# Layer 0 of a graph network: the edge-type one-hots by a broadcast load and a compare instead of a transpose on TensorE

## The chip, the cores and the metric

The kernel runs on one core of a Trainium2 chip. The metric is the time of one execution on the device in microseconds (us), as the median of several runs. The engines are named as the profile names them: PE (TensorE, matrix multiplies; PEld is its loading of weights), DVE (VectorE), ACT (ScalarE), POOL (GpSimd) and SP (SyncE, which here only issues DMAs).

## The reference

Four graph layers run one after the other on 3125 nodes of 256 features and 50,000 edges, sorted by destination. After each, the result is added to `x` and normalised. The change lies in layer 0, whose edge part is:

```python
e = edge_emb[edge_type]                       # 16 types
x_src, x_dst = node_embeddings[src], node_embeddings[dst]
att_in = concat([x_src, x_dst, e, task_rep], axis=-1)
edge_delta = tanh(gelu(att_in @ att_W1 + att_b1) @ att_W2 + att_b2)
edge_weight = 1.0 + edge_scale * edge_delta
messages = ((x_src + e) @ msg_W + msg_b) * (1.0 + 0.5 * tanh(msg_gamma)) + msg_beta
agg = segment_sum(messages * edge_weight, dst)     # then divided by the sum of edge_weight
```

Since `att_W1` acts on a concatenation, its product is a sum of a part by source, a part by destination and a part by edge type. The kernel computes the three parts per node and per type once and looks them up for each edge.

## The kernel before

**Tiles.** Edges are cut into 416 tiles (`TT`) of up to 128 edges, so that the destinations of one tile lie within one block of 128 nodes; four tiles are a group (`G`), and there are 104 groups. The function `bucket` prepares the tiles' data once: `s_src`, `s_dl` (destination within the block) and `s_ty` (type) hold one edge per partition and one tile per column. It also calls `segments`, which works on the transposed form (one tile per partition, edges along the columns) and makes the tables for the softmax of later layers. `segments` takes 128 tiles at a time, in four blocks, and collects a block's values in `pk`, one PSUM buffer of 128 x 4 x 128 float32 values, by matmuls with the selection matrix `sel`. Its third slice was used only for `kd`, one column (L380), which DVE reads as `low` (L383) before it goes on to `dl` (L388).

**One-hot matrices.** A look-up by destination is a matmul with a 0/1 matrix. `gathered` makes two of them per tile: `places[:, 0]` has a one in the column of each edge's destination (L928), and `places[:, 1]` has in columns 0 to 47 three copies of the type's one-hot over 16 types (L934, from the one made on L931), with zeros in the other 80 columns, set once (L918). PE turns both (L939), eight transposes per group into one PSUM buffer `ohp`, and ACT copies the 1024 columns to `oht` (L943). Three copies are needed since the per-type table `ec` holds its values as three bfloat16 parts under one another, 48 rows, padded with zeros to 128.

**The edge loop** runs `gathered` for one group, `attended` for the group before and `summed` for the one before that. POOL gathers the source rows into `gb` (L509, by `self.gather`). `attended` adds up the three parts in `pre` on PE: the source part by a matmul with the identity (L956, three bfloat16 parts), the destination part with `oht[:, 0]` (L961, three parts per tile), the type part with `oht[:, 1]` and `ec` (L964, one per tile). ACT applies Gelu (L965), DVE multiplies with `att_W2` and sums (L967). `summed` makes the weighted one-hots `ohw` (L972 to L976) and adds each tile's messages to `acc` (PE L979, DVE L981). The L979 matmuls are float32, all the others of the loop bfloat16.

For every second group SP stores the pair's destination one-hots and their transposes to memory (`oh_d`, `oht_d`, L946), where layers 1 and 2 load them.

**Order.** The kernel's source gives the order in which buffers are written and read; a planner with estimated costs sets the order of instructions on each engine and adds the waits. Each engine then works through its list in order. Access to a PSUM buffer is kept in order by the bank.

Of the kernel before, what the change touches and what calls it, by code (L numbers as in the profile page):

```python
# [9 lines left out]
F32 = mybir.dt.float32  # L10
# [8 lines left out]
P = 128  # L19
D = 256  # L20
# [13 lines left out]
class Net:  # L34
# [178 lines left out]
    def bucket(self, src, dst, type16, type8, weight, relations):  # L213
# [22 lines left out]
        self.seg = self.dram.tile([TT, 5, P], F32, name="seg")  # L236

        self.rows = self.dram.tile([NS, 2, S], F32, name="rows")
        self.astart, self.aend, self.anew = (c.tile([1, TT], F32, name=n) for n in ("astart", "aend", "anew"))
        self.tnode = c.tile([1, TT], I32, name="tnode")  # L240

        with tc.tile_pool(name="bk", bufs=1, side="right") as b:
# [40 lines left out]
            with tc.tile_pool(name="bkw", bufs=1, side="right") as w, tc.tile_pool(name="bkp", bufs=1, space=PSUM) as ps:  # L283
# [71 lines left out]
                nc.vector.tensor_single_scalar(bat, bat, D, op=ALU.mult)  # L355
                nc.scalar.dma_start(self.b_at, bat)

                self.segments(w, bd, nxt, prv, bdf, sel, kd)

    def segments(self, w, bd, nxt, prv, bdf, sel, kd):  # L360

        tc, nc, TT = self.tc, self.nc, self.TT
        C = bd.shape[1]
        flag = w.tile([P, 2, C, P], F32, name="flag")
        nc.vector.tensor_tensor(flag[:, 0], prv, bd, op=ALU.not_equal)
        nc.vector.tensor_tensor(flag[:, 1], nxt, bd, op=ALU.not_equal)
        zero = w.tile([P, P], F32, name="zero")
        nc.vector.memset(zero, 0.0)
        with tc.tile_pool(name="sgp", bufs=1, space=PSUM) as ps, tc.tile_pool(name="sg", bufs=2, side="right") as v:
            rows = ps.tile([1, 3, 512], F32, name="rows")  # L370
            for m0 in range(0, TT, P):
                M = min(P, TT - m0)
                pk = ps.tile([P, 4, P], F32, name="pk")
                for n in range(3):
                    for k in range(C):
                        nc.tensor.matmul(pk[:M, n, :], sel[:, k, m0:m0 + M],
                                         bdf[:, k, :] if n == 0 else flag[:, n - 1, k, :],
                                         start=k == 0, stop=k == C - 1)
                for k in range(C):
                    nc.tensor.matmul(pk[:M, 3, 0:1], sel[:, k, m0:m0 + M], kd[:, k:k + 1],  # L380
                                     start=k == 0, stop=k == C - 1)
                low = v.tile([P, 1], F32, name="low")
                nc.vector.tensor_scalar(low[:M], pk[:M, 3, 0:1], self.pidx[:M], float(m0),  # L383
                                        op0=ALU.add, op1=ALU.add)
                nc.vector.tensor_scalar(low[:M], low[:M], float(P), None, op0=ALU.mult)
                sg = v.tile([P, 5, P], F32, name="sg")
                dl = v.tile([P, P], F32, name="dl")
                nc.vector.tensor_scalar(dl[:M], pk[:M, 0, :], low[:M], None, op0=ALU.subtract)  # L388
                ins = v.tile([P, P], F32, name="ins")
                nc.vector.tensor_scalar(ins[:M], dl[:M], 0.0, None, op0=ALU.is_ge)  # L390
                nc.vector.scalar_tensor_tensor(ins[:M], dl[:M], float(P), ins[:M], op0=ALU.is_lt, op1=ALU.mult)
                nc.vector.tensor_scalar(sg[:M, 0], ins[:M], -1.0, -NEG, op0=ALU.add, op1=ALU.mult)
                for n in (1, 2):
                    nc.vector.scalar_tensor_tensor(sg[:M, n], pk[:M, n, :], NEG, ins[:M],
                                                   op0=ALU.mult, op1=ALU.mult)
                nc.vector.tensor_tensor_scan(sg[:M, 3], zero[:M], sg[:M, 1], 0.0, op0=ALU.add, op1=ALU.min)
                nc.vector.tensor_tensor_scan(sg[:M, 4, ::-1], zero[:M], sg[:M, 2, ::-1], 0.0,
                                             op0=ALU.add, op1=ALU.min)
                edge = v.tile([P, 1], F32, name="edge")
                nc.vector.tensor_add(edge[:M], sg[:M, 0, 0:1], sg[:M, 1, 0:1])  # L400
                for n, col in enumerate((sg[:M, 3, P - 1:P], sg[:M, 4, 0:1], edge[:M])):
                    nc.tensor.matmul(rows[:, n, m0:m0 + M], col, self.ident[:M, :M], start=True, stop=True)
                nc.sync.dma_start(self.seg[m0:m0 + M], sg[:M])
            for n, row in enumerate((self.astart, self.aend, self.anew)):
                nc.vector.tensor_copy(row, rows[:, n, :TT])
            rrow = w.tile([1, TT // S, 2, S], F32, name="rrow")
            nc.vector.memset(rrow, NEG)
            st, en = (r.rearrange("p (s t) -> p s t", t=S) for r in (self.astart, self.aend))
            nc.vector.tensor_copy(rrow[:, :, 0, 1:], st[:, :, :S - 1])
            nc.vector.tensor_copy(rrow[:, :, 1, :S - 1], en[:, :, 1:])  # L410
            nc.sync.dma_start(self.rows.rearrange("s n t -> (s n t)")[None, :], rrow.rearrange("p s n t -> p (s n t)"))
# [342 lines left out]
    def layer0(self, task, edge_emb, msg_W, msg_b, att_W1, att_b1, att_W2, att_b2, edge_scale,  # L754
# [9 lines left out]
        with ExitStack() as layer:  # L764
# [21 lines left out]
            ub2 = vec(up_b2, D, "ub2")  # L786
            lng = vec(ln_g, D, "lng")
            lnb = vec(ln_b, D, "lnb")
            ec = wp.tile([P, D], BF, name="ec")
            nc.vector.memset(ec, 0.0)  # L790
            one = wp.tile([P, 1], F32, name="one1")
            nc.vector.memset(one, 1.0)
            me = wp.tile([ET, D], F32, name="me")
# [2 lines left out]
            with tc.tile_pool(name="n0", bufs=2) as w, tc.tile_pool(name="m0", bufs=1) as wm, \  # L796
# [18 lines left out]

                ml = film_loads(ma_W1, ma_b1, ma_W2, ma_b2, "ma")
                ul = film_loads(ua_W1, ua_b1, ua_W2, ua_b2, "ua")
                E3 = 3 * ET
                emb = wm.tile([E3, D], F32, name="emb")
                for n in range(3):  # L820
                    nc.sync.dma_start(emb[n * ET:(n + 1) * ET, :], edge_emb)
# [58 lines left out]
                nc.vector.tensor_scalar(fst[:, 2:3], self.pidx[:E3], float(2 * ET), None, op0=ALU.is_ge)  # L880
                nc.vector.tensor_add(fst[:, 1:2], fst[:, 0:1], fst[:, 2:3])
                nc.vector.tensor_scalar(fst[:, 1:2], fst[:, 1:2], -1.0, 1.0, op0=ALU.mult, op1=ALU.add)
                nc.vector.tensor_scalar(ecs, part[:, 0, :], fst[:, 0:1], None, op0=ALU.mult)
                for n, o in ((1, ecs), (2, ec[:E3])):
                    nc.vector.scalar_tensor_tensor(o, part[:, n, :], fst[:, n:n + 1], ecs,
                                                   op0=ALU.mult, op1=ALU.add)
                nc.vector.tensor_add(me, mb[:ET, :], pc[:ET, 1, :])
# [23 lines left out]
            with tc.tile_pool(name="e0g", bufs=5) as gp, tc.tile_pool(name="e0", bufs=3) as w, \  # L911
# [1 line left out]

                places = [hp.tile([P, 2, 2, G, P], BF, name="places%d" % n) for n in range(2)]
                for n, oh in enumerate(places):
                    (nc.vector if n % 2 else nc.gpsimd).memset(oh[:, 1], 0.0)  # L918
                ohts = [None]

                def gathered(t0):
                    gb = gp.tile([P, G, ET + XA], F32, name="gb")
                    for j in range(G):
                        self.gather(gb[:, j, ET:], table, self.s_src, t0 + j)
                    g = t0 // G % 2
                    both = places[t0 // (2 * G) % len(places)]
                    oh = both[:, :, g]
                    nc.vector.tensor_tensor(  # L928
                        oh[:, 0], self.iota[:, None, :].to_broadcast([P, G, P]),
                        self.s_dl[:, t0:t0 + G][:, :, None].to_broadcast([P, G, P]), op=ALU.is_equal)  # L930
                    nc.vector.tensor_tensor(  # L931
                        gb[:, :, 0:ET], self.iota[:, None, :ET].to_broadcast([P, G, ET]),
                        self.s_ty[:, t0:t0 + G][:, :, None].to_broadcast([P, G, ET]), op=ALU.is_equal)
                    nc.vector.tensor_copy(oh[:, 1, :, 0:3 * ET].rearrange("p j (n e) -> p j n e", n=3),  # L934
                                          gb[:, :, None, 0:ET].to_broadcast([P, G, 3, ET]))
                    pt = ps.tile([P, 2, G, P], BF, name="ohp")
                    for n in range(2):
                        for j in range(G):
                            nc.tensor.transpose(pt[:, n, j, :], oh[:, n, j, :], self.idb)  # L939
                    if not g:  # L940
                        ohts[0] = hp.tile([P, 2, 2, G, P], BF, name="oht", bufs=2)
                    oht = ohts[0][:, :, g]
                    nc.scalar.copy(oht, pt)  # L943
                    if g:
                        for to, of in ((self.oh_d, both), (self.oht_d, ohts[0])):
                            nc.sync.dma_start(to[t0 // (2 * G)], of[:, 0].rearrange("p g j v -> p (g j v)"))  # L946
                    return t0, gb, oh, oht

                def attended(t0, gb, oh, oht):
                    hg = w.tile([P, G, D], F32, name="hg", bufs=2)  # L950
                    dl = w.tile([P, G], F32, name="dl")
                    for j0 in range(0, G, 2):
# [4 lines left out]
                        for j in (j0, j0 + 1):  # L957
                            q = pre[:, j - j0, :]
                            node = self.node_of(nc.tensor, t0 + j)
                            for n in range(3):  # L960
                                last = nc.tensor.matmul(q, oht[:, 0, j, :], xbr[:, ds(node * (3 * D) + n * D, D)],  # L961
                                                        start=False, stop=False)
                            self.used(nc.tensor, last)
                            nc.tensor.matmul(q, oht[:, 1, j, :], ec, start=False, stop=j > j0)  # L964
                        nc.scalar.activation(hg[:, j0:j0 + 2, :], pre, AF.Gelu)  # L965
                        for j in (j0, j0 + 1):
                            nc.vector.scalar_tensor_tensor(hg[:, j, :], hg[:, j, :], 1.0, aw2, op0=ALU.mult,  # L967
# [3 lines left out]
                def summed(t0, gb, oh, dl):  # L971
# [1 line left out]
                    nc.scalar.activation(dl, dl, AF.Identity, bias=one, scale=esc)  # L973
                    ohw = w.tile([P, G, P], F32, name="ohw", bufs=2)
                    for j in range(G):
                        nc.scalar.activation(ohw[:, j, :], oh[:, 0, j, :], AF.Copy, scale=dl[:, j:j + 1])  # L976
                    for j in range(G):
                        pa = ps.tile([P, SW], F32, name="pa", bufs=3)
                        nc.tensor.matmul(pa, ohw[:, j, :], gb[:, j, 0:ET + D], start=True, stop=True)  # L979
# [645 lines left out]
```

## Time and profile before

| what | value |
|---|---|
| time of the runs shown, median of 3 | 3369.55 us (3362.56 to 3373.93) |
| time of the profiled execution | 3362.1 us |
| its span, first to last instruction | 3360.3 us |
| mean granted TensorE clock | 0.843 of full speed |
| PE, DVE, ACT, POOL busy over the span | 80%, 68%, 43%, 54% |
| layer 0's edge loop | about 212 to 796 us, at granted clock 1.00 from 250 us on |
| transposes L939 / type matmuls L964 | 832 / 416 |
| gathers L509 in the loop | 416, mean 0.98 us |

A line such as `L964 PE MATMUL pre<-ec,oht 128*128 128x256 bf16` names the line of the kernel, the engine, what is written from what, and for PE the shape of the weights (rows*columns) and of the data that stream past them. In the timeline each line begins with the start and the length in microseconds; a group of neighbouring instructions is one line, with its number behind an x. The bracket at the end is the idle time of the engine ahead of it and what ended that; "issue" is idle time for which the profile shows no wait. Matmuls are pipelined: the length of one includes its way through the array, so what one costs PE is read from the distance of the starts.

### The profile page before, as it was taken

To read this page: it belongs to the slowest core of one execution; us is meant where nothing else is said; L and a number is where in the kernel's file an instruction comes from. 1 tells how busy PE (TensorE), PEld (TensorE's weight loads), DVE (VectorE), ACT (ScalarE), POOL (GpSimd) and SP (SyncE) were. 2 spreads that over 40 slices of the span, in tenths; PEclk is the share of its full clock that TensorE was granted. 3 is DMA by queue.
4 is the path that set the end of the run, shared out by engine and by line. 5 is a ranking of instruction groups with operands and counts; after the bars stand their busy time and mean duration, and the time that the engine had idled before them with its cause. 6 is when DMAs were issued, how large, how long until landed. Compare 5 with 4: busy or idle time off the path is not lost. (4 is left out here: it accounts for less than half of the span.)

```text
span 3360.3 us, 50557 instructions
## 1 busy us (share of the span) xinstructions
PE 2693.6 (80%) x12679; PEld 1753.9 (52%) x12679; DVE 2274.4 (68%) x6046; ACT 1446.9 (43%) x4376; POOL 1827.1 (54%) x1850
## 2 busy tenths in 40 slices
PE   2779999999979777777775847888888887888885
PEld 1357777775545345555553525666666663333332
DVE  2646666676655378988886437888888873555556
ACT  1427777774456335544543215656656562000000
POOL 4037767771044167666662556676766202777773
PEclk9889999999989878888887878888888985565656
DMA  7249988884067877777774367878777235333332
GB/s 167 72 147 295 295 284 289 287 291 137 32 252 288 311 225 244 232 230 238 228 229 136 116 206 201 225 225 227 228 226 228 76 140 215 105 105 106 106 105 86
DMA packets 240616, 658.40 MB, mean 196 GB/s; under 512 B 47960, under 2 KB 87012, under 8 KB 234013
## 3 DMA queue, kind: packets, MB, share of 16 engines
q0 software_dynamic: 132400, 484.37, 46.4%
q1 hardware_dynamic: 104262, 167.53, 15.1%
q10 hardware_dynamic: 3676, 3.23, 0.5%
q8 instruction: 122, 2.00, 0.2%
q14 instruction: 156, 1.28, 0.1%
HBM read 513.06 MB, written 151.58 MB: 198 GB/s over the span
## 5 line engine op out<-in xcount | busy, mean ns | idle before, releaser
L509 POOL DMA_INDIRECT gb<-table,s_src x832 | 852.4, 1025 | 374.8 <-issue 203.9
L706 PE MATMUL pr<-r,oh 128*128 128x260 f32 x2496 | 733.6, 440 | 80.7 <-DVE acc L711 32.9
L706 PEld LDWEIGHTS pr<-r,oh 128*128 128x128 f32 x2496 | 502.5, 217 | 216.0 <-issue 33.1
L1509 POOL DMA_INDIRECT ring<-table,b_rel x391 | 369.9, 946 | 312.8 <-DVE oh L1519 194.0
L701 ACT ACTIVATE r<-gb,ex 128x64 f32<-128x64 f32 x2080 | 522.4, 336 | 0.0
L509 POOL DMA_INDIRECT gb<-table,s_rel x416 | 405.4, 974 | 204.9 <-issue 106.0
L711 DVE TENSOR_TENSOR acc<-acc,pr 128x260 f32 (+1 forms) x832 | 457.7, 550 | 72.7 <-PE pr L706 60.8
L1538 PE MATMUL pa<-ring,oh 128*128 x832 | 428.9, 628 | 84.1 <-DMA ring<-table,b_rel 41.2
L1538 PEld LDWEIGHTS pa<-ring,oh 128*128 128x128 f32 x832 | 193.7, 283 | 319.6 <-DVE oh L1519 215.2
L1545 DVE TENSOR_TENSOR x<-x,pa 128x256 f32 x416 | 175.2, 421 | 227.0 <-PE pa L1538 225.2
L1237 PE MATMUL pqe<-q_all,oht 128*128 x1248 | 207.8, 306 | 91.9 <-DVE pd L1242 76.1
L693 ACT CAST oh<-ohb 128x512 f32<-128x512 bf16 x208 | 128.3, 618 | 307.2 <-PE pr L706 278.6
L589 ACT ACTIVATE r<-mv,eps 128x4 f32<-128x4 f32 (+3 forms) x27 | 7.9, 297 | 536.5 <-DVE mv L575 533.1
L697 DVE TENSOR_TENSOR r<-gb,ex 128x512 f32<-128x512 f32 (+1 forms) x208 | 225.8, 1086 | 12.9 <-ACT ex L666 9.2
L979 PE MATMUL pa<-gb,ohw 128*128 128x272 f32 x832 | 223.7, 402 | 5.3 <-DVE acc L981 3.8
L1237 PEld LDWEIGHTS <-oht 128*128 128x128 bf16 x1248 | 131.6, 107 | 126.8 <-issue 86.0
L961 PE MATMUL pre<-xb,oht 128*128 x1248 | 193.7, 273 | 0.0
L981 DVE TENSOR_TENSOR acc<-acc,pa 128x272 f32 x416 | 180.7, 434 | 6.2 <-PE pa L979 3.4
L928 DVE TENSOR_TENSOR places<-iota,s_dl 128x512 bf16<-128x512 f32 x104 | 72.0, 692 | 161.5 <-ACT ohw L976 161.5
L956 PE MATMUL pre<-gb,idb 128*128 128x512 bf16 x624 | 169.3, 381 | 5.3 <-DMA gb<-table,s_src 5.3
L979 PEld LDWEIGHTS pa<-gb,ohw 128*128 128x128 f32 x832 | 141.5, 190 | 55.6 <-issue 35.1
L967 DVE SCALAR_TENSOR_TENSOR hg<-hg,aw 128x256 f32<-128x256 f32 x416 | 159.4, 421 | 16.1 <-ACT hg L965 16.1
(381 smaller groups left out, 4291.6 us busy)
## 6 DMA issues: line engine op xcount, KB each, us to landing
ohb<-oh_d SPq DMA_DIRECT2D x104, 256.0 KB
oht<-oht_d SPq DMA_DIRECT2D x104, 256.0 KB
table<-row SPq DMA_DIRECT2D x25, 1024.0 KB
gb<-table,s_src POOLq DMA_INDIRECT x832, 4.5
oh_d<-places SPq DMA_DIRECT2D x52, 256.0 KB
oht_d<-oht SPq DMA_DIRECT2D x52, 256.0 KB
sgm<-seg SPq DMA_DIRECT2D x26, 320.0 KB
gb<-table,s_rel POOLq DMA_INDIRECT x416, 4.4
```

The lines of the kernel that those rows point to most:

```text
L509: self.nc.gpsimd.indirect_dma_start(out=out, out_offset=None, in_=table, in_offset=bass.IndirectOffsetOnAxis(ap=idx[:, t:t + 1], axis=0))
L697: nc.vector.tensor_mul(r[:, :, :nd, :hw], v[:, :, :nd, :], ex[:, :nd, s0:s0 + G].rearrange("p h t -> p t h")[:, :, :, None].to_broadcast([ ...
L701: nc.scalar.activation(r[:, j, h, :hw], v[:, j, h, :], AF.Copy, scale=ex[:, h, s0 + j:s0 + j + 1])
L706: nc.tensor.matmul(pr[:, n, :HB * F], oh[:, j, :], r[:, j, n * HB:(n + 1) * HB, :].rearrange("p h f -> p (h f)"), start=True, stop=True)
L711: self.used(nc.vector, nc.vector.tensor_add(a, a, pr[:, :, :HB * F]))
L961: last = nc.tensor.matmul(q, oht[:, 0, j, :], xbr[:, ds(node * (3 * D) + n * D, D)], start=False, stop=False)
L979: nc.tensor.matmul(pa, ohw[:, j, :], gb[:, j, 0:ET + D], start=True, stop=True)
L981: self.used(nc.vector, nc.vector.tensor_add(a, a, pa))
L1237: last = nc.tensor.matmul(pq[:, j, :], oht[:, j, :], q_all[:, ds(node * (3 * D) + n * D, D)], start=n == 0, stop=n == 2)
L1509: st = nc.gpsimd.indirect_dma_start(out=ring[:, at:at + D], out_offset=None, in_=table, in_offset=bass.IndirectOffsetOnAxis(ap=b_rel[:, b: ...
L1538: last = nc.tensor.matmul(pa, oh[:, j, :], ring[:, ds(at, D)], start=True, stop=True)
L1545: self.used(nc.vector, nc.vector.tensor_add(a, a, pa))
```

## The change

The transposed type one-hots are no longer made from `places[:, 1]`. `segments` now writes each tile's 128 types to memory (`ty_d`, one row per tile), taken by four more matmuls per block (L376's kind, in float32) into the slice `pk[:, 3, :]` after `low` has been read. In the loop, SP loads for each pair of groups the 1024 types, the same row into each of 48 partitions. In `attended`, DVE compares them with each partition's own type number `own` (0 to 15, three times over) in place, and the result is the weights of the type matmul: 48 rows instead of 128. `ec` and the one-hots lose their padding, `ohp` and `oht` their second half.

```diff
+        self.ty_d = self.dram.tile([TT, P], BF, name="ty_d")
...
+                for k in range(C):
+                    nc.tensor.matmul(pk[:M, 3, :], sel[:, k, m0:m0 + M], f16[:, k, :], start=k == 0, stop=k == C - 1)
+                ty = v.tile([P, P], BF, name="ty")
+                nc.scalar.copy(ty[:M], pk[:M, 3, :])
+                nc.sync.dma_start(self.ty_d[m0:m0 + M], ty[:M])
                 sg = v.tile([P, 5, P], F32, name="sg")
...
-            ec = wp.tile([P, D], BF, name="ec")
-            nc.vector.memset(ec, 0.0)
+            E3 = 3 * ET
+            ec = wp.tile([E3, D], BF, name="ec")
+            own = wp.tile([E3, 1], F32, name="own")
...
+                nc.vector.scalar_tensor_tensor(own, fst[:, 2:3], 2.0, fst[:, 1:2], op0=ALU.mult, op1=ALU.add)
+                nc.vector.scalar_tensor_tensor(own, own, -float(ET), self.pidx[:E3], op0=ALU.mult, op1=ALU.add)
...
-                places = [hp.tile([P, 2, 2, G, P], BF, name="places%d" % n) for n in range(2)]
-                for n, oh in enumerate(places):
-                    (nc.vector if n % 2 else nc.gpsimd).memset(oh[:, 1], 0.0)
-                ohts = [None]
+                both = [None]
 
                 def gathered(t0):
...
-                    both = places[t0 // (2 * G) % len(places)]
-                    oh = both[:, :, g]
+                    if not g:
+                        both[0] = [hp.tile([p, 2, G, P], BF, name=n, bufs=2) for p, n in (
+                            (P, "places"), (P, "oht"), (E3, "types"))]
+                        nc.sync.dma_start(both[0][2].rearrange("p g j e -> p (g j e)"), bass.AP(
+                            tensor=self.ty_d.tensor, offset=self.ty_d.offset + t0 * P,
+                            ap=[[0, E3], [1, 2 * G * P]]))
+                    oh, oht, ty = (b[:, g] for b in both[0])
...
-                    nc.vector.tensor_copy(oh[:, 1, :, 0:3 * ET].rearrange("p j (n e) -> p j n e", n=3),
-                                          gb[:, :, None, 0:ET].to_broadcast([P, G, 3, ET]))
-                    pt = ps.tile([P, 2, G, P], BF, name="ohp")
-                    for n in range(2):
-                        for j in range(G):
-                            nc.tensor.transpose(pt[:, n, j, :], oh[:, n, j, :], self.idb)
+                    pt = ps.tile([P, G, P], BF, name="ohp")
+                    for j in range(G):
+                        nc.tensor.transpose(pt[:, j, :], oh[:, j, :], self.idb)
...
-                def attended(t0, gb, oh, oht):
+                def attended(t0, gb, oh, oht, ty):
+                    nc.vector.tensor_scalar(ty, ty, own, None, op0=ALU.is_equal)
...
-                            nc.tensor.matmul(q, oht[:, 1, j, :], ec, start=False, stop=j > j0)
+                            nc.tensor.matmul(q, ty[:, j, :], ec, start=False, stop=j > j0)
```

## The prediction

> **What bounds the kernel now.** I looked first at the stages: where does the time go in which the changed code runs? The busy times by window (columns: PE, weight loads, DVE, ACT, POOL busy us with instruction counts, granted clock, DMA share, GB/s) give for 100 us in the middle of layer 0's edge loop:
>
> ```profile
> 450.00:550.00 100.00, 99.05 (x692) 71.76 (x690) 69.00 (x271) 71.61 (x164) 69.78 (x73) 1.00 0.89 287
> ```
>
> PE is busy 99 of 100 us at full clock; nobody else passes 72, though the DMA engines stand at 0.89. The loop runs from 212 to 796 us, 104 groups of four edge tiles. Next, the waits between 250 and 750 us (total, times, longest):
>
> ```profile
> DVE places L928 <- ACT ohw L976: 148.4, 91, 1.7
> ACT dl L972 <- DVE hg L967: 115.4, 91, 1.7
> ...
> PE pa L979 <- DVE acc L981: 2.3, 10, 0.4
> ```
>
> DVE and ACT wait once a group (91 groups, 1.6 and 1.3 us each), for one another and in the end for PE's `pre`; PE itself waits 2.3 us in 500. So a group costs what PE's instructions cost. "Busy" overlaps for pipelined matmuls, so I price by start-to-start times in PE's timeline (start, length, number):
>
> ```profile
> 500.90 2.10 PE L979 MATMUL pa<-gb,ohw 128*128 128x272 f32 x8
> ...
> 502.83 0.61 PE L939 MATMUL ohp<-idb,places 128*128 128x128 bf16 x8
> 503.28 0.81 PE L956 MATMUL pre<-gb,idb 128*128 128x512 bf16 x3
> 503.93 0.49 PE L961 MATMUL pre<-xb,oht 128*128 x3
> 504.26 0.27 PE L964 MATMUL pre<-ec,oht 128*128 128x256 bf16 x1
> 504.37 0.49 PE L961 MATMUL pre<-xb,oht 128*128 x3
> ...
> 506.32 2.10 PE L979 MATMUL pa<-gb,ohw 128*128 128x272 f32 x8
> ```
>
> A period is 506.32 - 500.90 = 5.42 us. Eight transposes take 503.28 - 502.83 = 0.45 us, 56 ns each; L964 takes 504.37 - 504.26 = 0.11 us, no more than each L961 (0.33/3). Loads of weights are hidden.
>
> **What is removed in the loop.** Four of the eight transposes: 4 x 0.056 = 0.225 us of PE per group. ACT's copy of 1024 columns (0.99 us) becomes one of 512; the nearest row, the 128x512 cast L693, has 0.62, so -0.37. DVE's cast L934 (0.27) goes. For the end this is worth nothing: both engines wait over a microsecond per group for PE, and without PE in the way DVE would still need only 5.42 - 1.65 = 3.8 us a group.
>
> **What L964 becomes.** It has 48 rows of weights instead of 128, four times a group, each time between 128-row matmuls. L964 is the step on which this forecast turns. The trace of before has no 48-row matmul, but it has 16-row and 64-row ones among 128-row ones. In layer 0's node stage (PE alone):
>
> ```profile
> 807.22 1.99 PE L1027 MATMUL pm<-sx,mw 128*128 128x512 f32 x4
> 809.14 1.12 PE L1029 MATMUL pm<-sx,me 16*128 16x512 f32 x2
> 810.19 1.42 PE L1012 MATMUL tr<-ident,acc 128*128 128x128 f32 x11
> ...
> 820.51 1.88 PE L1044 MATMUL pm<-gT,uw 128*128 128x512 f32 x4
> 822.23 1.88 PE L1044 MATMUL pm<-xT,uw 128*128 128x512 f32 x4
> ```
>
> Without a change of rows, four such matmuls take 822.23 - 820.51 = 1.72 us (0.43 each). With one they take 809.14 - 807.22 = 1.92, and the two of 16 rows 1.05 instead of 0.86: 0.2 us more per change. Half of that is a float32 weight load that is no longer pulled ahead (0.11), the rest, 0.09, is the array running empty. In bf16, in layer 1's loop, around a 64-row transpose:
>
> ```profile
> 1230.25 0.27 PE L1237 MATMUL pqe<-q_all,oht 128*128 x1
> 1230.45 0.27 PE L664 MATMUL mis<-ident,smA 64*128 64x64 f32 x1
> 1230.65 0.28 PE L1237 MATMUL pqe<-q_all,oht 128*128 x1
> 1230.78 0.41 PE L1237 MATMUL pqe<-q_all,oht 128*128 x2
> ```
>
> The bf16 matmul of 256 columns (0.11) gives way after 0.20: again 0.09 of emptying. Back at 128 rows the first bf16 matmul takes 0.12, so its exposed load costs only about 0.01. A change costs 0.10 with bf16 weights behind it and 0.09 + 0.11 = 0.20 with float32 weights.
>
> Against these rows stand two sentences of the Trainium skill. "TensorEngine Tiling (Array Packing)", Tiling Modes (Key Properties), says that a change of tiling mode drains the array; its modes have 128, 64 or 32 rows, so 48 rows would run as 64. "TensorE: Matmul & The Clock Gate", LDWEIGHTS, says that the number of rows does not matter for a load. By the second alone L964 costs its 0.11 as before; by the first and the rows it costs two changes. Both are true in the trace (16-row matmuls are no slower by themselves), and the first decides, because it is the neighbours that pay. That 48 counts as 64 no row shows; the 48-column matmul L872 is followed by a gap like the others ("issue" 0.40 before the next load), which I take as the same rounding.
>
> Per group: eight changes, 7 x 0.10 + 0.20 (the last L964 is followed by the float32 L979) = 0.90 us. With 0.225 less for transposes: **+0.67 us per group, 104 x 0.67 = +70 us**. Ends: if the 48-row bf16 weights load without the short path, each way in costs 0.20: +0.39 per group, +111 us in all; the page of the clock gate (Weight-path perf modes) ties that path to 128 columns and not float32, which L964 keeps, so I stay near the row. Below: no change of mode, -0.225 x 104 = -23.
>
> **The compare.** One per group, 48x512 bf16, on DVE ahead of L964. Nearest rows: tensor_scalar L312, 0.43 us for 416 float32 columns, and L928, 0.69 for 512; below, L390 at 0.23 for 128. I take 0.5. DVE is busy 0.69 of 5.42 = 3.7 us per group; 3.7 - 0.3 + 0.5 = 3.9 of 6.1: hidden. It waits for a load, and behind it on DVE stand `hg`, `acc` and the next one-hots, for which ACT and then PE wait: with DVE's idle time (1.65 a group now, about 2.2 then) it takes a load some 4 us late per pair of groups before PE feels it.
>
> **The load and the stores.** 52 loads of 48 rows x 2 KB on SP. The hardware queue moved 12973 packets in 500 us at 12.4% of 16 engines: 76 ns each. 48 x 76 / 16 = 0.23 us per pair, 2% of 10.84. Share 0.91 at the old pace, 0.81 at the slower one: no bound. SP issues three DMAs of 0.32 us per pair instead of two. It does stand up to 9.7 us a pair in front of the `oht_d` store, waiting for ACT; a load queued behind it leaves late, but it is asked for a group before its use, and gathers beside it land in 4.5 us. I cost it at nothing. Stores behind a load wait only for tile reuse two pairs on.
>
> **Ahead of the loop.** `segments` is on the path: the loop's first one-hot starts (211.8) after its last copies. Four blocks each get eight float32 matmuls of 128 columns, an ACT copy and a store. L376's sixteen take 1.95 us, so eight take 0.98, behind DVE's `low`; `dl` then waits, since all of `pk` is one bank (in layer 1 L644 waits for ACT's copy of another part of its bank, 24 times). `dl` starts 0.24 us after the first `low` ends; with load, eight matmuls and tail of 0.17 it starts about 1.3 after: +1.1 per block, x4 = 4.4; at half clock, as in the second block, up to 8; 0 if the planner hides it. The copy (0.4) and store lie beside DVE's 2 us. Removed: POOL's memset L918, 1.1 us in front of the first gather (0 to 1.1 won; I take 0.5). The two small DVE operations for `own` lie among node tiles: 0. Net **+4**.
>
> **Sum.** 70 + 4 = +74 us. The profiled execution took 3362.1 (span 3360.3 and 1.8 around it), so 3436; the median of the runs shown is 7.5 above it, so 3369.55 + 74 = **3444**. The bound of 0.3%, which a measurement here can tell from nothing, is 10 us.
>
> **Rivals.** (1) *48 rows change no mode.* Then -23 + 4 = -19: 3350, faster. POOL (1.22 us a gather, 4.9 a group) and DMA (0.91 x 5.42 = 4.9) allow 5.2. For it: the row-count sentence. Against it: every row-count change in the trace pays. With p for a change it wins where 8p + 0.10 + 4/104 is under 0.225: p below 0.01 us, a tenth of what the rows show. 9%. (2) *Dearer loads*, the 0.20 above: +111 + 4, 3485; 14%. (3) *Some changes are free*, say half: +0.22 per group, +23 + 4, 3397; 7%. (4) *The load lands late*: at 2 us beyond the slack, 52 x 2 = 104 more, 3548; gathers' landing speaks against it. 4%. My forecast has 66%, own range 3425 to 3465.
>
> **Range and chances.** 3395 to 3490 takes all of the first, most of (2) and part of (3): 80%. It leaves out (1) and (4). Faster 0.09, within 0.3% 0.01, slower 0.90.
>
> **What will show it.** Period of L979 about 6.1 us; the loop's stage about 70 us longer, with DVE, ACT and DMA shares down and PE still never waiting. Weight loads of the 48-row matmul and of those after it starting about 0.09 after the stream of the one before, "issue" ahead of them. Transposes 416, not 832. Blocks of `segments` a microsecond longer each. Wrong if PE's starts around the 48-row matmul stay 0.11 apart, or if PE idles for DVE's compare.

## The result

The kernel after the change takes 3430.3 us (median of four runs, 3423.0 to 3431.2), the kernel before 3368.7 (3362.6 to 3373.9): a ratio of **1.0185** (95% interval 1.017 to 1.020), 61.6 us slower. The profiled executions are 68.1 us apart (3430.2 and 3362.1), at granted clocks of 0.849 and 0.843.

In three of the five sets of runs below the kernel before itself took about 4040 us instead of 3365, since signals from TensorE reached the other engines up to 2.5 us late and TensorE no longer bounded the loop ("late signals" below); every ratio is therefore to the kernel before in its own set, and those three sets are read for TensorE's start-to-start times more than for their totals.

### The profile after

The stage first: busy times by window, for the same 100 us of the edge loop as in the prediction (PE, weight loads, DVE, ACT, POOL, then granted clock, DMA share, GB/s).

```profile
450.00:550.00 100.00, 99.93 (x563) 58.03 (x563) 66.48 (x247) 56.74 (x150) 73.67 (x66) 1.00 0.87 268
```

PE is still the bound, with 563 matmuls in 100 us instead of 692. From the first L986 (L979 before) to the end of the last one the loop takes 624.3 us (239.7 to 864.0) instead of 567.2, and the median distance between groups is 6.03 us instead of 5.43. Next, PE's own timeline of one group (start, length):

```profile
504.07 0.28 PE L971 MATMUL pre<-ec,types 48*128 48x256 bf16 x1
504.29 0.50 PE L968 MATMUL pre<-xb,oht 128*128 x3
504.72 0.28 PE L971 MATMUL pre<-ec,types 48*128 48x256 bf16 x1
504.93 0.82 PE L963 MATMUL pre<-gb,idb 128*128 128x512 bf16 x3
...
506.66 0.28 PE L971 MATMUL pre<-ec,types 48*128 48x256 bf16 x1
506.87 0.50 PE L986 MATMUL pa<-gb,ohw 128*128 128x272 f32 x1
```

Behind each type matmul (L971, L964 before) the next one starts 0.21 us later, where it was 0.11; ahead of it the last L968 takes 0.205 until L971 starts. The waits between 300 and 780 us (total, times, longest) say what PE's weight loads sit idle for, and whether PE waits for anyone:

```profile
ACT hg L972 <- PE pre L971: 105.5, 79, 1.3
...
PEld L971 <- issue: 66.7, 317, 0.2
...
DVE types L956 <- DMA types<-ty_d: 49.1, 40, 1.8
...
PEld pa L986 <- issue: 5.2, 12, 0.7
...
PE pa L986 <- DVE acc L988: 0.3, 1, 0.3
```

Ahead of each of 317 loads of 48-row weights PEld idles 0.21 us, with no wait to blame. DVE waits 1.2 us per pair of groups for the types' load (40 pairs), and PE feels little of it: the loads for L986 stand idle 12 times, and by the starts of L986 every second distance is longer than 6.03 by 0.09 us in the mean, 4.5 us in the whole loop.

By the first L986 10.3 us more have passed than before by the first L979: 1.9 before `segments` starts (I have no cause for it; over all the traces kept that moment lies anywhere between 174.5 and 183.3 us), 7.8 in `segments` from its first matmul to the last `dl` (36.0 instead of 28.2), the rest at the loop's start. The timeline of one block of `segments`:

```profile
183.72 1.16 PE L389 MATMUL pk<-f,sel 128*128 128x128 f32 x8
...
184.91 0.27 ACT L391 CAST ty<-pk 128x128 bf16<-128x128 f32 x1 [7.10 <-PE pk L389]
...
185.21 0.35 DVE L395 TENSOR_SCALAR dl<-pk,low 128x128 f32<-128x128 f32 x1 [1.25 <-ACT ty L391]
```

DVE's `dl` waits not only for the eight type matmuls, but also for ACT's copy out of the same bank. After the loop nothing changed (2563.6 us before, 2564.4 after).

### The profile page after: what moved, and what is told of

Read it like the earlier page. It is cut to its first block, busy times and chain, and to the rows that moved or that the text cites. A ratio compares the mean times of both kernels' runs of the same rounds, so it can differ in the third digit from the quotient of the medians.

```text
span 3428.4 us, 49867 instructions
## 1 busy us (share of the span) xinstructions
PE 2753.0 (80%) x12295; PEld 1708.0 (50%) x12295; DVE 2293.7 (67%) x6046; ACT 1394.9 (41%) x4380; POOL 1876.9 (55%) x1849
## 5 line engine op out<-in xcount | busy, mean ns | idle before, releaser
L516 POOL DMA_INDIRECT gb<-table,s_src x832 | 902.5, 1085 | 519.1 <-issue 210.7
L986 PE MATMUL pa<-gb,ohw 128*128 128x272 f32 x832 | 222.9, 407 | 1.4 <-DVE acc L988 1.2
L968 PE MATMUL pre<-xb,oht 128*128 x1248 | 207.2, 275 | 0.0
L972 ACT ACTIVATE hg<-pre 128x512 f32<-128x512 f32 x208 | 123.5, 594 | 146.0 <-PE pre L971 146.0
L986 PEld LDWEIGHTS pa<-gb,ohw 128*128 128x128 f32 x832 | 145.8, 189 | 46.8 <-issue 7.3
```

The lines of the kernel that those rows point to most:

```text
L516: self.nc.gpsimd.indirect_dma_start(out=out, out_offset=None, in_=table, in_offset=bass.IndirectOffsetOnAxis(ap=idx[:, t:t + 1], axis=0))
L968: last = nc.tensor.matmul(q, oht[:, j, :], xbr[:, ds(node * (3 * D) + n * D, D)], start=False, stop=False)
```

## The experiments

Theory M is the prediction's: every 48-row matmul among 128-row ones costs two changes of row mode. Theory L says that the types' load, the comparison or the DMA traffic costs the time; theory S says `segments` does. Rival G, for the versions with a faster TensorE, says that the gathers would then be late.

### The type matmul alone cut to 48 rows

```diff
-                            nc.tensor.matmul(q, oht[:, 1, j, :], ec, start=False, stop=j > j0)
+                            nc.tensor.matmul(q, oht[:3 * ET, 1, j, :], ec[:3 * ET], start=False, stop=j > j0)
```

> The kernel before, with one thing of the change alone: the type matmul (L964) takes the first 48 rows of its weights and of ec; transposes, copies, casts and segments stay. Theory M (each 48-row matmul among 128-row ones is two changes of row mode, about 0.10 us each, eight per group): the median distance of two L979 starts goes from 5.43 to 5.43 + 0.82 = 6.25 us, and the time, less some 5 us that the first groups already lose to late gathers, from 3369 to about 3450 (3440 to 3457). Theory L (the time is lost to the types load, its comparison on DVE or the extra DMA traffic, none of which is in this kernel): 3369 and 5.43. Theory S (the segments' extra work is the main cost): 3369.

Measured: ratio 1.0003 (0.9975 to 1.003), in a set where the kernel before took 4040 us. What went on there is seen best in its 80-row sister, whose expectation was:

> As the 48-row version of the kernel before, but with 80 rows, of which rows 48 to 79 are zero as before. Theory M with 48 rows running as a 64-row mode and 80 as the full 128: no change of mode, 3369 us and a distance of 5.43. Rival M' (any row count other than 128 empties the array on both sides): the same as 48 rows, about 3450 and 6.25. Theory L or S: 3369, so this run only says which row counts pay.

The edit is the same with `5 * ET`; the ratio is 0.9986 (0.9962 to 1.001). From the timeline of this 80-row kernel, one group:

```profile
502.45 0.27 PE L964 MATMUL pre<-ec,oht 80*128 80x256 bf16 x1
...
502.56 1.54 PE L979 MATMUL pa<-gb,ohw 128*128 128x272 f32 x6
...
505.27 0.60 ACT L965 ACTIVATE hg<-pre 128x512 f32<-128x512 f32 x1 [2.52 <-PE pa L979]
505.32 0.44 DVE L981 TENSOR_TENSOR acc<-acc,pa 128x272 f32 x1 [1.62 <-PE pa L979]
```

L964 was done at 502.7, yet ACT, idle, starts on its result at 505.27; in the trace of before the same hand-over took 0.04 us. DVE starts at the same moment on a result that PE had finished at 503.2. PE has run out of buffers meanwhile. A group takes 7.40 us here in both kernels. Where signals are prompt (below) it takes 5.43 with 128 rows and 6.25 with 48, so what M adds is spent inside a wait here. Busy times by window, first the kernel with 80 rows, then with 48:

```profile
450.00:550.00 100.00, 74.85 (x509) 52.97 (x507) 56.00 (x201) 52.89 (x121) 51.07 (x54) 1.00 0.69 212
```

```profile
450.00:550.00 100.00, 88.03 (x512) 49.89 (x511) 55.85 (x200) 53.11 (x122) 51.58 (x55) 1.00 0.69 212
```

PE is 13 us of 100 busier for the same work and the same pace. The start-to-start times are clean: with 48 rows 0.205 us into the type matmul and 0.212 out of it (medians of 416 and 208), with 80 rows 0.109 and 0.113. So 80 rows beside 128 change no mode, and 48 do. This agrees with the Trainium skill, "TensorEngine Tiling (Array Packing)", Tiling Modes (Available Configurations), where the modes have 128, 64 or 32 rows; its Key Properties name the drain, and the price, 0.10 us each way, comes from these rows. A rival, that the 48-row loads are merely not pulled ahead, would make the way out longer where a longer load follows; it is 0.21 us before the bf16 loads (98 ns) and before the float32 ones (190 ns) alike. The totals of this pair decide nothing between M and L. A repetition, with its expectation:

> The same kernel as k48_alone (before, with the type matmul alone cut to 48 rows), since on the first chip signals from TensorE reached the other engines late and TensorE waited in both kernels. On a chip where the kernel before takes about 3369 us, theory M expects what it did: a distance of 6.25 us, and about 3450 us (3440 to 3457); theories L and S: 3369. On a chip where the kernel before takes about 4040 us again, theory M expects no difference in time, and TensorE about 0.8 us a group busier.

came out under the same condition: 1.0005 (0.9978 to 1.0032), distance 7.41.

### The same with the gathers left out

The next two runs were meant to make TensorE the bound again under late signals.

```diff
+                gbs = [gp.tile([P, G, ET + XA], F32, name="gb%d" % n, bufs=1) for n in range(5)]
...
-                    gb = gp.tile([P, G, ET + XA], F32, name="gb")
-                    for j in range(G):
-                        self.gather(gb[:, j, ET:], table, self.s_src, t0 + j)
+                    gb = gbs[t0 // G % 5]
+                    if t0 < 5 * G:
+                        for j in range(G):
+                            self.gather(gb[:, j, ET:], table, self.s_src, t0 + j)
```

> The kernel before with 396 of layer 0's 416 gathers left out: the five buffers of gathered rows are filled once and used again and again, so layer 0's sums are of the wrong rows; every other instruction of the loop stays. In the seven traces of this kind of chip TensorE's signals are late (by up to 2.5 us, several at once) only in stretches where GpSimd issues gathers. If the gathers bring that on, the loop is bound by TensorE again: 5.42 us from L979 to L979, a loop of about 104 x 5.42 = 564 us instead of 760, and a time of about 4043 - 196 = 3847 (3835 to 3860). If the signals are late whatever GpSimd does, the distance stays at 7.4 and the time near 4043, and no kernel of this study can be bound by TensorE on such a chip.

The condition had passed: the kernel before took 3360.9 us in this set and this kernel 3363.2, ratio 0.9998 (0.9984 to 1.0012). So whether gathers bring on the late signals stays open; what the run shows is that layer 0's gathers cost the kernel before little. Its loop is 8 us shorter (559.1), and that is not a late start: of the 8.5 us that the kernel before loses against 5.43 us a group, the first ten distances hold 1.6, and nearly all of it lies in every second distance, all through the loop. There DVE's first `acc` of a group starts late, behind the sequencer's reading of the next node numbers:

```profile
L523 DVEq TENSOR_LOAD <-tnode x87: 339/345/1006, 302.0 to 775.2; - x87
```

The three numbers are the shortest, the median and the longest in ns (300 to 780 us); without the gathers none is over 345 there. In every second distance of the kernel before, the distance follows the length of this read (correlation 0.94).

> The kernel few_gathers_before (396 of layer 0's 416 gathers left out, so the sums are of the wrong rows) with the type matmul cut to 48 rows. few_gathers_before took 0.9998 of the kernel before (3363 and 3361 us), so the gathers are hidden there, and leaving them out keeps the loop bound by TensorE whether signals are prompt or late. Theory M: 5.43 + 0.82 = 6.25 us from group to group, 104 x 0.82 = 86 us, 1.0253 of few_gathers_before: 3448 us where the kernel before takes 3361 (3440 to 3455). Theories L (load, comparison or traffic of the types) and S (segments): 3363, since none of that is in this kernel.

Measured: **1.0250** (1.0233 to 1.0267) of the kernel before, and so 1.0252 of few_gathers_before by way of its 0.9998, where 1.0253 was expected; the distance is 6.25 us in nearly every group, against 5.43. The groups of the type matmul between 300 and 780 us (busy, mean ns, idle before), first with 128 rows, then with 48:

```profile
L967 PE MATMUL pre<-ec,oht 128*128 128x256 bf16 x354 | 96.5, 273 | 0.0
L967 PEld LDWEIGHTS <-oht 128*128 128x128 bf16 x354 | 34.7, 98 | 4.0
```

```profile
L967 PE MATMUL pre<-ec,oht 48*128 48x256 bf16 x306 | 85.6, 280 | 0.0
L967 PEld LDWEIGHTS <-oht 48*128 48x128 bf16 x306 | 28.3, 93 | 64.4 <-issue 64.4
```

Matmul and load are as long as before; only the 0.21 us of idle time ahead of each load is new. M alone gives more than the whole loss of the change (the loop is 83 us longer than in few_gathers_before), and there is no load, no comparison and no extra work in `segments` here. L and S are out as the main cause; what is left of L in the kernel after is the 4.5 us above, and of S the 7.8.

### The two 48-row matmuls of a pair put together

```diff
                             self.used(nc.tensor, last)
-                            nc.tensor.matmul(q, ty[:, j, :], ec, start=False, stop=j > j0)
+                        for j in (j0, j0 + 1):
+                            nc.tensor.matmul(pre[:, j - j0, :], ty[:, j, :], ec, start=False, stop=j > j0)
```

> The kernel after, with the two 48-row matmuls of each pair of tiles put behind one another (after the one-hot matmuls of both tiles), so that a group has four changes of row mode instead of eight. Theory M: 4 x 0.105 = 0.42 us less per group, a distance of 5.61 instead of 6.03, and 3430 - 44 = 3387 us (3380 to 3395). If instead each 48-row matmul has a price of its own, whatever stands beside it, the time stays near 3430. Theory L: 3430.

Under late signals: 0.9936 (0.9908 to 0.9964). PE's starts were as M says: 0.205 into the first of the two, 0.119 between them, 0.202 out. Then again:

> The same kernel as paired (after, with the two 48-row matmuls of a pair of tiles one behind the other, four changes of row mode a group instead of eight). Where the kernel before takes about 3361 us, theory M: 5.61 us from group to group and 3423 - 0.42 x 104 = 3379 us (3372 to 3386), 1.0033 to 1.0075 of the kernel before; theory L: 3423, 1.0185. Where it takes about 4040: 0.9936 again.

1.0095 (1.0074 to 1.0117). Even distances (from the first group to the second, from the third to the fourth, and so on) are 5.61 us, exactly as expected: 0.42 less with four changes of mode fewer, so the price belongs to the change and not to the matmul. But the gain in time, 0.9% or 30 us, is short of the expected 44. (That it is about half of the whole loss is chance, since the loss has other terms too.) Odd distances say where the rest is: 5.88 in the median and 5.95 in the mean, 0.34 x 51 = 17 us. Once per pair something else is now the limit. The last kernel of the next section shows it plainly.

### Every matmul on 128 rows

```diff
-            ec = wp.tile([E3, D], BF, name="ec")
+            ecp = wp.tile([P, D], BF, name="ec")
+            nc.vector.memset(ecp, 0.0)
+            ec = ecp[:E3]
...
+                types = [hp.tile([P, 2, G, P], BF, name="types%d" % n) for n in range(2)]
+                for ty in types:
+                    nc.vector.memset(ty, 0.0)
...
-                    nc.vector.tensor_scalar(ty, ty, own, None, op0=ALU.is_equal)
+                    nc.vector.tensor_scalar(ty[:E3], ty[:E3], own, None, op0=ALU.is_equal)
...
-                            nc.tensor.matmul(q, ty[:, j, :], ec, start=False, stop=j > j0)
+                            nc.tensor.matmul(q, ty[:, j, :], ecp, start=False, stop=j > j0)
```

> The kernel after, with the types tile held on 128 partitions in two fixed buffers, zero in rows 48 to 127, loaded and compared in rows 0 to 47 only, and ec padded with zero rows to 128, so that every matmul of the loop has 128 rows; loads, comparison and segments stay. Theory M: the distance of two L979 starts falls from 6.03 to 5.43 - 0.22 = 5.20 us, and the time to about 3352 (3345 to 3362), below the kernel before by the transposes (104 x 0.225 = 23 us) less the 8 us of the segments. Rival G (with TensorE that fast the gathers are late, as in the first groups of the kernel before): the distance stays near 5.4 and the time near 3372, with TensorE waiting for DMA. Theory L: 3425 to 3435, hardly below the kernel after. Theory S: the same.

> The same kernel as pad128 (after, with every matmul on 128 rows). Where the kernel before takes about 3369 us: theory M, a distance of 5.20 us and about 3352 us (3345 to 3362); rival G (gathers late), 5.4 us and 3372; theories L and S, 3425 to 3435. Where it takes about 4040 us again: 0.985 to 0.995 of the kernel before.

Both runs came under late signals: 0.9896 (0.9838 to 0.9954) and 0.9933 (0.9910 to 0.9956), distances from 5.1 to 9 us. For comparison, the kernel after itself in that condition:

> The kernel after itself, on a chip of the kind that ran the last six kernels. If TensorE's signals are late here again (the kernel before near 4040 us, 7.4 us a group, of which TensorE works 5.3), theory M says that the 0.6 us a group more on TensorE lies inside the wait: not 1.0185 of the kernel before, but 0.990 to 1.003 (4000 to 4055 us), with one-hot and type matmuls starting 0.205 and 0.212 us after one another as in every run so far. If the change cost something beside TensorE's row modes (the load, the comparison), it would have to show here too: above 1.01. On a chip where the kernel before takes about 3369 us: 3430 again.

0.9968 (0.9945 to 0.9990): slower by 1.85% where PE bounds the loop, but 0.3% faster where waits do. M foresaw that nothing would show here; a wait for the load could lie hidden in the same wait, so the run does not exclude one. Where the 0.3% comes from I can't show.

The last version adds to `pad128` another way of making the types for memory:

```diff
-                for k in range(C):
-                    nc.tensor.matmul(pk[:M, 3, :], sel[:, k, m0:m0 + M], f16[:, k, :], start=k == 0, stop=k == C - 1)
-                ty = v.tile([P, P], BF, name="ty")
-                nc.scalar.copy(ty[:M], pk[:M, 3, :])
-                nc.sync.dma_start(self.ty_d[m0:m0 + M], ty[:M])
...
+                p = ps.tile([P, 4, P], F32, name="pty_t", tag="pick", bufs=3)
+                ty = w.tile([P, 4, P], BF, name="ty")
+                for n, m0 in enumerate(range(0, TT, P)):
+                    M = min(P, TT - m0)
+                    nc.tensor.transpose(p[:M, n, :], self.s_ty[:, m0:m0 + M], self.ident)
+                    nc.scalar.copy(ty[:M, n, :], p[:M, n, :])
+                    nc.sync.dma_start(self.ty_d[m0:m0 + M], ty[:M, n, :])
+
                 self.segments(w, bd, nxt, prv, bdf, sel, kd, f16)
```

> The kernel after with two edits: every matmul of the loop on 128 rows (types padded with zero rows, as in pad128), and the types for memory not made in the segments' blocks but turned there from the types by edge (four transposes of s_ty before the segments, four copies on ACT to bf16, four stores). Theory M, and my reading of the segments (in each block DVE's dl waits 1.33 us more, for the type matmuls and for ACT's copy out of the same bank): dl starts 0.22 us after low again instead of 1.55, the stretch from the segments' first matmul to the last dl is shorter by 5 to 8 us than in pad128, and the time is 5 to 8 us below pad128's: on a chip with late signals 0.985 to 0.994 of the kernel before, on one where it takes 3369 us about 3345 us. If the segments' extra time lies elsewhere (the clock, the stores), dl comes early but the stretch stays.

0.9911 (0.9879 to 0.9943) under late signals, where 5 to 8 us can't be told apart: `pad128` had 0.9896 and 0.9933. The part about `segments` is read from the trace: `dl` starts 0.22 us after `low` in all four blocks instead of 1.55, and the stretch is 25.9 us, where the kernels that make the types in the blocks take 32.4 to 36.0 and those that make none 25.3 to 29.7. So the segments' cost lies in what waits in the blocks, and it is avoidable (the four transposes stand ahead of that stretch, some 0.6 us by the row of L349). Once more, with prompt signals:

> The same kernel as pad_and_turned_types (after, with every matmul on 128 rows, and the types for memory turned before the segments). Where the kernel before takes about 3361 us, theory M: 5.20 us from group to group, less than the kernel before by 23 us in the loop and by 2 in the segments, if the gathers keep up: 3336 to 3345 us, 0.9925 to 0.9955. If the gathers are late at that pace (rival G), 5.4 us and 3358, the same as before. Where the kernel before takes about 4040: 0.991 again.

**A miss: 1.0052** (1.0034 to 1.0069), 13 us above the kernel before by the medians, instead of 15 to 25 below. `segments` is fine (24.4 us), and so are the even distances, 5.10 us each. The odd ones are 6.17. The waits of this kernel between 300 and 780 us:

```profile
DVE types L964 <- DMA types<-ty_d: 62.7, 42, 1.9
PEld pa L994 <- issue: 53.6, 43, 1.7
...
PE pa L994 <- DVE acc L996: 36.4, 43, 1.3
...
POOL gb L519 <- DMA gb<-table,s_src: 9.4, 31, 0.3
```

43 pairs, 43 waits of PE for DVE. From its timeline, one of them:

```profile
451.08 0.32 SPq L944 DMA_DIRECT2D types<-ty_d  x1
...
455.32 0.35 DVE L964 TENSOR_SCALAR types<-types,own 48x512 bf16<-48x512 bf16 x1 [1.81 <-DMA types<-ty_d]
...
455.59 0.42 DVE L996 TENSOR_TENSOR acc<-acc,pa 128x272 f32 x1
455.94 1.28 DVE L948 TENSOR_TENSOR places<-iota,s_dl 128x512 bf16<-128x512 f32 x2
...
458.10 0.42 DVE L996 TENSOR_TENSOR acc<-acc,pa 128x272 f32 x1
...
458.67 0.70 PE L994 MATMUL pa<-gb,ohw 128*128 128x272 f32 x2 [1.14 <-DVE acc L996]
```

DVE stands 1.8 us for the types' load; `acc` and the next one-hots queue behind it, and PE's L994 for the fourth tile finds none of the three `pa` buffers free until 458.67. Over the pairs the odd distance follows the length of DVE's wait for the types (correlation 0.96). It is not rival G: no wait of PE for a gather is in the list. Why the load is late is told by SyncE's own waits, here of the kernel after:

```profile
SPq L936 <- PE pre L971: 235.0, 40, 6.1
```

SP holds the load until PE has done the last type matmul of the pair that used the buffer two pairs before (the load at 264.39 us leaves 0.03 after it). The comparison starts 3.8 us after that issue in the median (here at 268.21), as early as the load allows, though its first matmul comes only at 279.58: the planner has put it early on DVE. A third buffer for the types, or the comparison further back in DVE's list, should free both. My estimate, with 5.10 us for every group: the loop would take 103 x 5.10 + 2 = 527 us, 40 less than before. That was not tried.

## Why the prediction was right, and where not

The direction and the cause were right, and 3444 stands 14 us above the 3430 measured. That is close in part by luck: in the traces the loop came out 13 us below its forecast and the part ahead of it 6 above. By its steps:

- **What bounds the loop**: right in the main. PE is at 99.9 of 100, and nobody's relief counted: ACT fell from 71.6 to 56.7 us of 100 for nothing. But "a group costs what PE's instructions cost" was off by 0.10 us: in the kernel before PE waited that long for DVE in every group (see the eight changes below).
- **Transposes, -0.225 a group**: right. The distance with 48 rows and all eight transposes is 6.25, with four 6.03.
- **Eight changes of mode, +0.90**: right in kind, and right in size for each of them. Four ways in cost 0.096 each (0.205 - 0.109), three ways out 0.103 and then 0.011 for the exposed bf16 load, the last one 0.101 and then 0.101 for the exposed float32 load (0.333 between the first two L986, where L979 had 0.232): 0.93 together. Yet the distance grew by 0.82 only, since a wait of 0.10 that the kernel before had went away. Its lines, and then one of after:

```profile
501.72 0.43 DVE L981 TENSOR_TENSOR acc<-acc,pa 128x272 f32 x1
...
502.27 0.30 PEld L979 LDWEIGHTS pa<-gb,ohw 128*128 128x128 f32 x2 [0.26 <-issue]
```

```profile
507.63 0.44 DVE L988 TENSOR_TENSOR acc<-acc,pa 128x272 f32 x1 [1.12 <-PE pa L986]
```

  There are three `pa` buffers, so the fourth tile's L979 must wait for the first tile's `acc`. Before, that `acc` stood behind two L967 in DVE's queue, and in all of the 88 groups looked at (12 to 99) the seventh of the eight L979 starts 0.146 to 0.148 us after `acc` ends: 0.10 us lost between the sixth and the eighth. After, `acc` waits for PE instead, and in 73 of 88 groups the seventh comes about 0.28 us after its end, with no gap. Hence 1.93 us from the first L979 to the first transpose before and 1.94 after, for different reasons. So +0.60 a group instead of +0.67, and 103 x 0.60 = 62 us.
- **The loop's total, +70**: measured +57. Of the 62 another 4 go off because the odd distances of the kernel before are 8.1 us above their pace in all (the late `acc` shown with few_gathers_before), against 4.5 after; the rest is at the loop's ends. The 5 us that the later expectations put down to late gathers in the first groups are this.
- **48 rows count as 64**: that 48 change the mode and 80 don't is measured; which mode 48 rows run in isn't. L872, named for it, has 48 columns and all 128 rows, and says nothing of rows.
- **The ends**: "no change of mode" (rival 1) and "half of them free" (3) fall with 0.205 and 0.212 at every one of them, "dearer loads" (2) with the way in of 0.096, where it had 0.20.
- **`segments`, +4**: measured +7.8 in the two traces. The step that failed is "the copy and store lie beside DVE's 2 us": `dl` waits for ACT's copy too, since both read one bank, so it is 1.33 us a block instead of 1.1, 5.3 in four. The other 2.5 go with the granted clock: over the stretch it is 0.82 before and 0.76 after. In paired_again, which makes the types in the same way, it is 0.85; worked out from these, before and paired_again both have about 10 us at half clock in the stretch, and take 28.2 and 33.6 us, 5.4 apart, while after has about 17.
- **Comparison**: 0.37 us, not 0.5; hidden, as said.
- **"It takes a load some 4 us late per pair of groups before PE feels it"**: wrong, though the total hardly shows it. At 5.10 us a group a wait of 1.5 us on DVE costs PE 1.07 us a pair; at 5.61, where it is 1.2, it costs 0.34; at 6.03, with 1.2 again, 0.09. I had summed DVE's idle time over the group, but a wait at one place of its queue holds back what PE needs next. Nor did I see that the load waits for its buffer. Rival 1 is touched as well: without mode changes the time would not have been 3350, but above the 3381 of the last run, which has the cheaper `segments` besides.

## What to carry to other kernels

A matmul of 48 rows is no cheaper here than one of 128 (280 and 273 ns long), and beside 128-row ones it costs about 0.10 us on the way in and as much on the way out: pad the rows with zeros (80 rows were already free of it; in this kernel the late load then took the gain), or put the narrow matmuls next to one another. Idle time of an engine, summed over a period, is not slack for every wait: what stands behind that wait in the engine's queue is held back with it. An engine that is 99% busy can still be waiting a little each time, and a slower one hides that wait. And two costs in one loop can hide each other: the mode changes covered all but 4.5 us of the late load, so undoing them won 49 us (3430 to 3381) where the sum of the parts promised 85 to 94.

## What the runs showed of the hardware beyond that

- Signals from TensorE to the other engines can be late for whole runs. In three sets they came in bursts, often some 2.5 us after the matmul had ended, while DVE's signal back to PE was not late (L979 for the fourth tile starts 0.15 us after `acc` in the 80-row trace, as in the trace of before); the kernel before took 4040 us instead of 3365. It isn't the chip: one and the same chip ran a set of each kind. In the traces it is seen where GpSimd issues gathers, though not wherever it does (between 1100 and 1800 us of the 80-row trace they are issued and signals are prompt), and that the gathers cause it was not shown.
- Two 48-row matmuls in succession start 0.119 us apart, 128-row ones 0.109, so nearly all of the cost lies in the change of rows.
- DVE's sequencer reads the node numbers in 0.34 us where layer 0's gathers are left out, and in up to 1.0 us where they run.
- With every matmul on 128 rows a group took 5.10 us, not the 5.43 - 0.22 = 5.20 of the transposes: the eight float32 matmuls go through in 2.00 us instead of 2.10. In these even groups `acc` comes early enough, and the 0.10 us that PE waited for it before is gone.
